# A graph attention layer on one core: the node stages at both ends in blocks of four, edge attributes by the pair, and the target rows as three bf16 parts in the one-hot product

## The chip, the cores and the metric

The kernel runs on one core of one Trainium2 chip. The metric is the device time of one execution in microseconds (us). All 400,000 edges and all 12,500 nodes are worked on by that one core, and every operand and result lies in the chip's DRAM before and after.

## The reference: what is computed

One pre-normalised graph attention layer with N = 12500 nodes, E = 400000 edges, C = 128 channels and H = 8 heads. The edges come sorted by their target `dst`. Cut to what matters:

```python
h = relu(layernorm(x))                                   # [N, 128]
msg = (h @ w_src + b_src)[src] + (h @ w_dst)[dst]         # [E, 128]
rad = mlp(edge_attr_32)                                  # 32 -> 64 -> 64 -> 128, silu between
m   = (msg * edge_weight1 * rad) @ w_sep + b_sep          # [E, 256]: per head 16 for alpha, 16 value
alpha = smooth_leaky_relu(m[.., :16]); value = m[.., 16:]
att = segment_softmax((alpha * alpha_dot).sum(-1), dst)  # per target node and head
out = segment_sum(value * att, dst)                       # [N, 128]
result = x + out @ w_proj + b_proj
```

## The kernel before

**Node stage** (L144 to L290). x is loaded in 7 groups of 14 blocks of 128 rows (97 full blocks and one of 84 rows). For each group, `stats` (L191) computes mean and variance on DVE and their scale and shift, `norm` (L204) makes h = relu(scale * x + shift) on ACT, and `products` (L212) takes four blocks at a time: PE transposes them (L220), DVE copies the transposes out (L223), PE multiplies each block with [w_src | w_dst] (L230), and two blocks at a time are evicted, the source half by an ACT copy (L237) and the target half by a DVE add that brings in b_src (L238). After 14 blocks the two halves are stored to the DRAM tables `t_src` and `t_dst` on SP's queue (L244). In the second group `ends_and_cuts` marks where neighbouring edges differ in their target, tests that the edges are sorted and the windows narrow (`bad`), and stores the sections' first and last targets. These come from four loads of 400 single words each, `base` and `last`, on SP's queue (L167, L168).

**Main loop** (`windows` L603, `passes` L644). The value `bad` is read back and the fast path is taken. `windows` loads the small MLP weights into block-diagonal tiles and computes `tgt`, `far`, `w_s` and `b_s`; then the edges go by in 400 pairs. A pair k is 1000 edges, two sections of 500, eight tiles of 125. All edges of a section have targets within 64 rows from its first one, its window. The order is written out by hand: `step(k)` issues the following, and each engine executes its own part in that order.

- Loads on SP: edge weights broadcast to 128 partitions (`load_w`, 500 KB) and the 64 target rows of each section's window (`load_md`, from `t_dst`) for pair k+3, targets of two pairs (`load_d`), edge attributes (`load_e`: 8 DMAs for 8 pairs, spread over the steps).
- `gather(k+4)`: eight indirect DMAs on POOL (L718), each fetching 125 rows of `t_src`. The tile `gs` has four buffers, so the gather for pair k+4 waits until the transposes of pair k (L770) have read theirs.
- `mlp3(k)`: PE L758 into `p3`, DVE L761 adds the bias and multiplies with the edge weight to `rad`.
- `message(k)`: PE transposes the gathered rows into the bank `pm` (L770) and adds the target rows onto it as a one-hot product, `md` [64 rows x 128] times `ohT` [64 x 500] in f32 (L775); DVE multiplies `pm` with `rad` to mT (L779).
- `alphas(k, 0)`, `alphas(k, 1)`: PE L783, ACT silu L785, DVE L787 give `al`, the alpha halves of the two sections.
- `values(c, f)` and `sums(c)` for the pair c = k - 12: PE L864 and DVE L866 weight the values with the softmax numerators, PE L875 sums them over the edges of each target into the bank `misc`, and ACT evicts it to `ob` (L879). `ob` is stored to `agg` (overlapping windows) and `win`.
- `mlp1(k+2)` (L736, L739), `mlp2(k+1)` (L744, L746), `one_hot_T(k+1)` (DVE L751), `e_T(k+3)` (L728, L730), and in every odd step `scores` (PE L794 into `misc`, ACT L797 to `Sp`) for two pairs. The softmax of eight pairs runs in the steps with k mod 8 = 1, 2, 3; the indices of 16 pairs are prepared in the steps with k mod 16 = 8.

The PSUM bank `misc` exists once and is shared by the indices, the scores, the softmax's transposes and the sums, so the scores of an odd step wait until ACT has evicted the sums before them. The value stage runs 12 pairs behind (LAG), and after pair 399 there are 14 more steps, in which the partial sums of targets that cross sections are combined and scattered to `agg` by indirect DMAs.

**Final stage** (L1126 to L1200). In 7 groups of 14 blocks: `agg` is loaded, POOL adds b_out to x (L1162), DVE computes the quotients (L1165 to L1168), PE transposes them (L1179), ACT copies them out (L1182), PE multiplies with w_proj (L1186), DVE adds a bias row where the node has edges (L1185) and then the sum to x (L1190), and the group is stored.

Of the kernel before, what the change touches and what calls it, by code (L numbers as in the profile page):

```python
# [53 lines left out]
EP = 8  # L54
# [3 lines left out]
def gnn_kernel(ctx: ExitStack, tc: tile.TileContext, a: dict, out: bass.AP):  # L58
# [18 lines left out]
    agg = dram.tile([N + W, ROW], F32, name="agg")  # L77
    win = dram.tile([NS * W, ROW], F32, name="win")
    base_d = dram.tile([2, NP], I32, name="base_d")
# [15 lines left out]
    x_v = x[0:NF * P, :].rearrange("(p t) c -> p t c", t=NF)  # L95
    ident = const.tile([P, P], F32, name="ident")
# [48 lines left out]
    with tc.tile_pool(name="node", bufs=2) as np_, tc.tile_pool(name="node1", bufs=1) as n1, \  # L145
# [6 lines left out]
        b_nodes = n1.tile([P, C], F32, name="b_nodes")  # L152
        nc.scalar.dma_start(out=b_nodes, in_=a["b_src"].to_broadcast([P, C]))
# [6 lines left out]
        last = n1.tile([1, 2, NP], I32, name="last")  # L160
# [3 lines left out]
        nc.sync.dma_start(out=prev[1:RP, :], in_=dst[RC - 1:E - 1].rearrange("(p c) -> p c", c=RC))  # L164
        with nc.allow_non_contiguous_dma(reason="the sections' ends"):
            for f in range(2):
                nc.sync.dma_start(out=base[:, f, :], in_=dst_h[f:f + 1, :, 0])  # L167
                nc.sync.dma_start(out=last[:, f, :], in_=dst_h[f:f + 1, :, SEC - 1])  # L168
# [16 lines left out]
        spans = groups[:-1] + [(groups[-1][0], NB)]  # L185
        hs = {}

        def rows(t):
            return P if t < NF else tail

        def stats(g):  # L191
            t0, t1 = spans[g]
# [11 lines left out]
        def norm(g):  # L204
            t0, t1 = spans[g]
            hs[g] = np_.tile([P, XG, C], F32, name="h")
            for t in range(t0, t1):
                n = rows(t)
                nc.scalar.activation(hs[g][:n, t - t0, :], x_all[:n, t, :], AF.Relu,
                                     bias=shift[:n, t:t + 1], scale=rstd[:n, t:t + 1])  # L210

        def products(g):  # L212
            t0, t1 = spans[g]
            ms = np_.tile([P, 2, XG, C], F32, name="ms")
            for u0 in range(t0, t1, 4):
                us = range(u0, min(u0 + 4, t1))
                pt = nps.tile([P, 4, P], F32, name="pt")
                for u in us:
                    n = rows(u)
                    nc.tensor.transpose(pt[:, u - u0, :n], hs[g][:n, u - t0, :], ident[:n, :n])  # L220
                hT = np_.tile([P, 4, P], F32, name="hT")
                w = (len(us) - 1) * P + rows(us[-1])
                nc.vector.tensor_copy(hT.rearrange("p u n -> p (u n)")[:, :w],  # L223
                                      pt.rearrange("p u n -> p (u n)")[:, :w])
                for v0 in range(0, len(us), 2):
                    vs = us[v0:v0 + 2]
                    pm = nps.tile([P, 2, 2, C], F32, name="pm", bufs=4)
                    for j, u in enumerate(vs):
                        n = rows(u)
                        nc.tensor.matmul(pm[:n, j], hT[:, u - u0, :n], w_nodes, start=True, stop=True)  # L230
                    i, m = vs[0] - t0, len(vs)
                    if rows(vs[-1]) == P:
                        cuts = [(P, 0, m)]
                    else:
                        cuts = [(P, 0, m - 1)] * (m > 1) + [(tail, m - 1, m)]
                    for n, j0, j1 in cuts:
                        nc.scalar.copy(ms[:n, 0, i + j0:i + j1, :], pm[:n, j0:j1, 0, :])  # L237
                        nc.vector.tensor_tensor(  # L238
# [999 lines left out]
```

## Time and profile before

| | us |
|---|---|
| runs of the kernel | 6549.27, 6550.76, 6562.26; median 6550.76 |
| profiled execution | 6566.2, its span 6564.2, mean granted TensorE clock 0.873 |
| start, up to the first gather | 0 to 215.9 |
| gathers | 215.9 to 6259 |
| last steps, combination, scatter | 6259 to 6417.7 |
| final stage | 6417.7 to 6564.2 |

The profile is of one execution. PE is TensorE (matmuls), PEld its weight loads, DVE VectorE, ACT ScalarE, POOL GpSimd and SP SyncE, which issues most DMAs here. A group of instructions is given by line, engine, operation, and the tiles it writes and reads; f32 matmuls appear as two records each, so that L775, two products in each step, has 1600 records for 400 pairs. "Idle before" is the time the engine stood still in front of an instruction, with the instruction whose signal ended it. The granted clock is a share of the full TensorE clock.

### The profile page before, as it was taken

What the parts mean: (1) busy time and instruction counts of PE and PEld (TensorE: products, weight loads), DVE (VectorE), ACT (ScalarE), POOL (GpSimd) and SP (SyncE); (2) the same over time, 40 slices, a digit from 0 to 9 for tenths busy, and PEclk for the clock granted to TensorE, in tenths of its full rate; (3) what the DMA queues carried; (4) which work ended last, traced back from release to release, by engine and by line L of the source; (5) the groups of instructions that cost most, each with busy time, mean ns of one, the idle gap of its engine ahead of it and who ended that gap; (6) DMA issues with size and microseconds to landing.
All of it is one profiled execution on the core that took longest, in us unless ns stands there. A gap on an engine that the chain in (4) does not pass through costs nothing. (4 is left out here: it accounts for less than half of the span.)

```text
span 6564.2 us, 79188 instructions
## 1 busy us (share of the span) xinstructions
PE 5066.2 (77%) x26490; PEld 2665.6 (41%) x26490; DVE 2887.1 (44%) x5210; ACT 1785.1 (27%) x3797; POOL 3111.5 (47%) x3231
## 2 busy tenths in 40 slices
PE   3477878787878878788788787887887878888774
PEld 2234444444444444444444444444444444444453
DVE  4234444444444444444444444444444444444465
ACT  3122222222222222222222222222222222222221
POOL 0455555455554545544455454454554545545402
PEclk7688898898998989988888898898888989888885
DMA  3454444444444444444444444444444444444423
GB/s 124 135 144 119 124 119 115 125 117 121 121 122 118 121 119 119 124 117 115 123 120 121 119 116 121 122 115 120 121 117 122 119 120 121 124 119 118 114 60 123
DMA packets 884920, 783.25 MB, mean 119 GB/s; under 512 B 527255, under 2 KB 773279, under 8 KB 884250
## 3 DMA queue, kind: packets, MB, share of 16 engines
q1 hardware_dynamic: 778482, 560.72, 31.0%
q0 software_dynamic: 102816, 210.37, 13.6%
q10 hardware_dynamic: 3202, 6.99, 0.3%
q8 instruction: 212, 3.47, 0.2%
q14 instruction: 208, 1.70, 0.1%
HBM read 643.82 MB, written 134.27 MB: 119 GB/s over the span
## 5 line engine op out<-in xcount | busy, mean ns | idle before, releaser
L718 POOL DMA_INDIRECT gs<-t_src,idx x3200 | 3067.4, 959 | 3189.3 <-PE pm L770 1756.2
L787 DVE SCALAR_TENSOR_TENSOR al<-pa,sl 128x500 f32<-128x500 f32 x800 | 542.9, 679 | 1570.9 <-ACT sl L785 1022.1
L761 DVE SCALAR_TENSOR_TENSOR rad<-p,c_fc_b,w_b 128x500 f32<-128x500 f32 x800 | 553.6, 734 | 1389.4 <-PE p L758 1102.0
L783 PE MATMUL pa<-mT,c_w_a 128*128 128x500 f32 x1600 | 833.7, 603 | 256.8 <-DVE mT L779 248.1
L785 ACT ACTIVATE sl<-pa,c_b_a 128x500 f32<-128x500 f32 x800 | 541.4, 677 | 1789.4 <-PE pa L783 626.9
L864 PEld LDWEIGHTS V<-c_w_v,mT 128*125 128x125 f32 x6208 | 741.2, 188 | 634.8 <-issue 337.9
L864 PE MATMUL V<-c_w_v,mT 128*125 128x128 f32 x6208 | 891.3, 286 | 23.2 <-issue 1.1
L794 PE MATMUL misc<-al,w_s 128*32 128x500 f32 x1600 | 365.9, 986 | 539.5 <-ACT ob L879 525.3
L779 DVE TENSOR_TENSOR mT<-pm,rad 128x500 f32<-128x500 f32 x800 | 504.3, 672 | 280.1 <-PE pm L775 252.8
L758 PE MATMUL p<-h,w3b 64*128 64x500 f32 x1600 | 625.5, 870 | 0.0
L770 PEld LDWEIGHTS pm<-ident,gs 125*128 125x128 f32 x3200 | 430.1, 169 | 435.9 <-issue 435.9
L866 DVE TENSOR_TENSOR pvx<-V,Pem 125x512 f32<-125x512 f32 x776 | 528.9, 682 | 44.4 <-PE m L744 26.5
L770 PE MATMUL pm<-ident,gs 125*128 125x125 f32 x3200 | 533.6, 321 | 0.0
L875 PEld LDWEIGHTS misc<-pvx,oh 125*64 125x64 f32 x6400 | 365.5, 137 | 322.4 <-issue 279.7
L875 PE MATMUL misc<-pvx,oh 125*64 125x136 f32 x6400 | 473.0, 287 | 28.2 <-DVE pvx L866 27.6
L783 PEld LDWEIGHTS pa<-mT,c_w_a 128*128 128x128 f32 x1600 | 269.5, 191 | 500.6 <-DVE mT L779 287.4
L775 PE MATMUL pm<-ohT,md 64*128 64x500 f32 x1600 | 471.0, 656 | 0.1
L739 ACT ACTIVATE h<-p,b 128x500 f32<-128x500 f32 x400 | 270.5, 676 | 700.9 <-PE pa L783 157.2
L879 ACT COPY ob<-misc 128x136 f32<-128x136 f32 x400 | 108.7, 272 | 1292.5 <-remote 630.5
L744 PE MATMUL m<-h,w2b 128*128 128x500 f32 x800 | 449.6, 644 | 0.0
L728 PE MATMUL m<-ident,e_t 125*128 125x125 f32 x800 | 187.4, 319 | 204.4 <-ACT h L746 169.8
L746 ACT ACTIVATE h<-m,b 128x500 f32<-128x500 f32 x400 | 270.7, 677 | 223.4 <-PE m L744 55.0
(145 smaller groups left out, 3153.1 us busy)
## 6 DMA issues: line engine op xcount, KB each, us to landing
w_b<-in_edge_weight SPq DMA_DIRECT2D x400, 500.0 KB
d_b<-in_dst SPq DMA_DIRECT2D x400, 250.0 KB
gs<-t_src,idx POOLq DMA_INDIRECT x3200
e_t<-in_edge_attr SPq DMA_DIRECT2D x400, 125.0 KB
sc_d<-Sp SPq DMA_DIRECT2D x200, 250.0 KB
win<-ob SPq DMA_DIRECT2D x400, 68.0 KB
agg<-ob SPq DMA_DIRECT2D x800, 33.5 KB
md<-t_dst SPq DMA_DIRECT2D x800, 32.0 KB
```

The lines of the kernel that those rows point to most:

```text
L718: nc.gpsimd.indirect_dma_start(out=gs[:, j, :], out_offset=None, in_=t_src[:, :], in_offset=bass.IndirectOffsetOnAxis(ap=idx[:, t:t + 1], ...
L758: nc.tensor.matmul(p3[:, f, 0:SEC], w3b[s, :], h2s[k][s, :], start=True, stop=True)
L761: nc.vector.scalar_tensor_tensor(rads[f], p3[:, f, 0:SEC], b3, w_g[k][:, f * SEC:(f + 1) * SEC], op0=ALU.add, op1=ALU.mult)
L770: nc.tensor.matmul(pm[f][:, t * T:(t + 1) * T], gs[:T, f * TS + t, :], ident[:T, :T], start=(t == 0), stop=False, is_transpose=True, skip_ ...
L775: nc.tensor.matmul(pm[f], md[k][s, :], ohT[k][s, :], start=False, stop=True, skip_group_check=True)
L779: nc.vector.tensor_mul(mTs[k][:, f * SEC:(f + 1) * SEC], pm[f], rads[f])
L783: nc.tensor.matmul(pa, w_a, mTs[k][:, f * SEC:(f + 1) * SEC], start=True, stop=True)
L785: nc.scalar.activation(sl, pa, AF.Silu, bias=b_a, scale=1.0)
L787: nc.vector.scalar_tensor_tensor(al, pa, 0.25, sl, op0=ALU.mult, op1=ALU.add)
L864: nc.tensor.matmul(V[:, t, :], mTs[c][:, o:o + T], w_v, start=True, stop=True)
L866: nc.vector.tensor_mul(pvx[c][:, f, :, 0:C].rearrange("p t (h k) -> p t h k", h=H), V.rearrange("p t (h k) -> p t h k", h=H), Pem[c // MP] ...
L875: nc.tensor.matmul(acc[f * W:(f + 1) * W, :], ohs[c][:, f * TS + t, :], pvx[c][:, f, t, :], start=(t == 0), stop=(t == TS - 1), skip_group ...
```

## The change

1. *Node stage.* 25 quads of four blocks. `norm(i+2)`, `turn(i+1)` (transposes and their copy) and `products(i)` are issued in this order; `stats` are made for eight blocks at a time. Two blocks are evicted in one copy with both halves, on ACT, and one pair in eight on DVE; b_src is no longer added. Each quad is stored by itself. The sections' first and last targets are loaded as 1600 words by one DMA into 100 partitions (`ends`); of the four loads of 400 words the two of `base` stay. The MLP weights, `w_s`, `b_s`, `tgt`, `far` and the final stage's bias row `v_out` are loaded or computed here. `fits` (the test and the stores of `ends`) runs after quad 12 and `cuts` after the last one.
2. *b_src in the message.* mT = (pm + b_src) * rad, one scalar_tensor_tensor instead of a product.
3. *Edge attributes.* One DMA for each pair, six steps ahead, four buffers. The four tiles' order in a section changes with it: h1 is written permuted and `rad` strided, in one tile of 1000 columns with one buffer.
4. *Target rows.* `ohT` is written in bf16. `md` is split one step ahead into three bf16 parts that sum to it exactly (`split_md`, two ACT copies and two DVE subtractions of 128x128), and the one-hot product is six bf16 matmuls instead of two f32 ones.
5. *x + b_out.* `load_x` and `add_x` compute it in the loop, a quad in every eighth step from step 40 on, and store it to a DRAM table `xb`.
6. *Final stage.* x comes from `xb`; quotients for 12 blocks at a time; `turn(i+1)` is issued ahead of `finish(i)`; the result is made in place and stored for each quad. POOL does nothing.

The diff, cut to its core:

```diff
-        last = n1.tile([1, 2, NP], I32, name="last")
+        ends = n1.tile([100, 8, 2], I32, name="ends")
...
                 nc.sync.dma_start(out=base[:, f, :], in_=dst_h[f:f + 1, :, 0])
-                nc.sync.dma_start(out=last[:, f, :], in_=dst_h[f:f + 1, :, SEC - 1])
+            nc.sync.dma_start(out=ends, in_=bass.AP(
+                at.tensor, at.offset, [[8 * SEC, 100], [SEC, 8], [SEC - 1, 2]]))
...
+        def norm(i):
+            t0, t1 = quads[i]
+            hs[i] = np_.tile([P, 4, C], F32, name="h", bufs=3)
...
+        def products(i):
+            t0, t1 = quads[i]
+            hT = hTs.pop(i)
+            ms = np_.tile([P, 2, 4, C], F32, name="ms", bufs=4)
+            for v0 in range(t0, t1, 2):
+                vs = range(v0, min(v0 + 2, t1))
+                pm = nps.tile([P, 2, 2, C], F32, name="pm", bufs=4)
+                for t in vs:
+                    n = rows(t)
+                    nc.tensor.matmul(pm[:n, t - v0], hT[:, t - t0, :n], w_nodes, start=True, stop=True)
+                for n, u0, u1 in blocks(v0, vs[-1] + 1):
+                    o, q = ms[:n, :, u0 - t0:u1 - t0, :].rearrange("p k j c -> p j k c"), pm[:n, u0 - v0:u1 - v0]
+                    if v0 % 16 == 2:
+                        nc.vector.tensor_copy(o, q)
                     else:
-                        nc.scalar.copy(ms[:n, 0, i + j0:i + j1, :], pm[:n, j0:j1, 0, :])
-                        nc.vector.tensor_tensor(
-                            ms[:n, 1, i + j0:i + j1, :], pm[:n, j0:j1, 1, :],
-                            b_nodes[:n].unsqueeze(1).to_broadcast([n, j1 - j0, C]), op=ALU.add)
+                        nc.scalar.copy(o, q)
             f1 = min(t1, NF)
             for k, table in enumerate((t_src, t_dst)):
                 tv = table[0:NF * P, :].rearrange("(p t) c -> p t c", t=NF)
-                nc.sync.dma_start(out=tv[:, t0:f1, :], in_=ms[:, k, 0:f1 - t0, :])
+                if t0 < f1:
+                    nc.sync.dma_start(out=tv[:, t0:f1, :], in_=ms[:, k, 0:f1 - t0, :])
...
+        for i in range(Q):
+            if i % 2 == 0 and 4 * i + G < NB:
+                stats(4 * i + G, min(4 * i + 2 * G, NB))
+            if i + 2 < Q:
+                norm(i + 2)
+            if i + 1 < Q:
+                turn(i + 1)
+            products(i)
+            if i == 12:
+                fits()
+        cuts()
...
-            def load_e(g, i):
...
+            def load_e(k):
+                e_g[k] = lp.tile([T, 8, RAD], F32, name="e_t", bufs=4)
+                nc.sync.dma_start(out=e_g[k], in_=ea_t[k])
...
+            def split_md(k, i):
+                if i == 0:
+                    m3[k] = lp.tile([P, 3, C], BF16, name="m3")
+                    nc.scalar.copy(m3[k][:, 0, :], md[k])
+                elif i == 1:
+                    mr[k] = lp.tile([P, C], F32, name="mr")
+                    nc.vector.tensor_sub(mr[k], md.pop(k), m3[k][:, 0, :])
+                elif i == 2:
+                    nc.scalar.copy(m3[k][:, 1, :], mr[k])
+                else:
+                    nc.vector.tensor_sub(m3[k][:, 2, :], mr.pop(k), m3[k][:, 1, :])
...
-                nc.scalar.activation(h1s[k].rearrange("p (q e) -> p q e", q=2), p1[:, :, 0:2 * T],
+                nc.scalar.activation(h1s[k].rearrange("x (f q p) -> x q f p", f=2, q=2),
+                                     p1[:, :, 0:2 * T].rearrange("x q (f p) -> x q f p", f=2),
...
-                ohT[k] = sp.tile([P, SEC], F32, name="ohT")
+                ohT[k] = sp.tile([P, SEC], BF16, name="ohT")
...
-                rads = [sp.tile([C, SEC], F32, name="rad", bufs=3) for _ in range(2)]
...
+                rad = sp.tile([C, PR], F32, name="rad", bufs=1)
+                v = "x (t h p) -> x h t p"
+                n = dict(t=4, h=2)
+                for h in range(2):
+                    nc.vector.scalar_tensor_tensor(
+                        rad.rearrange(v, **n)[:, h], p3[:, h, 0:SEC].rearrange("x (t p) -> x t p", t=4),
+                        b3, w_g[k].rearrange(v, **n)[:, h], op0=ALU.add, op1=ALU.mult)
...
-                for f in range(2):
-                    s = slice(f * W, (f + 1) * W)
-                    nc.tensor.matmul(pm[f], md[k][s, :], ohT[k][s, :], start=False, stop=True,
-                                     skip_group_check=True)
+                for j in range(3):
+                    for f in range(2):
+                        s = slice(f * W, (f + 1) * W)
+                        nc.tensor.matmul(pm[f], m3[k][s, j, :], ohT[k][s, :], start=False, stop=(j == 2),
+                                         skip_group_check=True)
...
-                    nc.vector.tensor_mul(mTs[k][:, f * SEC:(f + 1) * SEC], pm[f], rads[f])
+                    s = slice(f * SEC, (f + 1) * SEC)
+                    nc.vector.scalar_tensor_tensor(mTs[k][:, s], pm[f], b_n, rad[:, s], op0=ALU.add, op1=ALU.mult)
...
+                if has(k + 6) and k >= -4:
+                    load_e(k + 6)
...
+                i, q = divmod(k - 40, MP)
+                if 0 <= i < Q and q == 5:
+                    load_x(i)
+                if 0 <= i < Q and q == 7:
+                    add_x(i)
                 if has(k + 4):
                     gather(k + 4)
+                if has(k + 1):
+                    split_md(k + 1, 0)
                 if has(c):
                     sums_begin(c)
                 if has(k):
                     message(k, mlp3(k))
                 if has(c):
                     values(c, 0)
+                if has(k + 1):
+                    split_md(k + 1, 1)
                 if has(k):
                     alphas(k, 0)
+                if has(k + 1):
+                    split_md(k + 1, 2)
                 if has(c):
                     values(c, 1)
...
                     one_hot_T(k + 1)
+                    split_md(k + 1, 3)
...
-                nc.gpsimd.tensor_tensor(x_all[:n, t0 + a0:t0 + a1, :], x_all[:n, t0 + a0:t0 + a1, :],
-                                        b_out[:n].unsqueeze(1).to_broadcast([n, a1 - a0, C]), op=ALU.add)
...
+        for i in range(Q):
+            if i % 3 == 0 and i // 3 + 3 < NG:
+                load_g(i // 3 + 3)
+            if i % 3 == 1 and i // 3 + 1 < NG:
+                quotients(i // 3 + 1)
+            if i + 1 < Q:
+                turn(i + 1)
             finish(i)
```

## The prediction, made before the changed kernel was run

> **What bounds the kernel now.** The page's first part names no engine that is full:
>
> ```profile
> PE 5066.2 (77%) x26490; PEld 2665.6 (41%) x26490; DVE 2887.1 (44%) x5210; ACT 1785.1 (27%) x3797; POOL 3111.5 (47%) x3231
> ```
>
> PE is the busiest at 77%, so the first question is whether PE's work sets the step. The costliest groups (busy us, mean ns, then the idle time before them) and the waits say otherwise:
>
> ```profile
> L718 POOL DMA_INDIRECT gs<-t_src,idx x3200 | 3067.4, 959 | 3189.3 <-PE pm L770 1756.2
> ...
> L775 PE MATMUL pm<-ohT,md 64*128 64x500 f32 x1600 | 471.0, 656 | 0.1
> ```
>
> ```profile
> POOL gs L718 <- PE pm L770: 1756.2, 235, 11.7
> ...
> ACT ob L879 <- remote: 630.5, 181, 4.7
> ...
> PE misc L794 <- ACT ob L879: 525.3, 144, 4.3
> ```
>
> POOL does nothing in the loop but issue gathers, is busy 3067 us and waits for the transposes of `message` (L770) 1756 us. PE in its turn waits 525 us at the scores (L794) for `ob`, the eviction of the sums' bank, and `ob` waits for something "remote" or for PE lines that have nothing to do with it. The timeline of two steps (start, duration, engine, line; in brackets the idle time and its releaser) shows the circle:
>
> ```profile
> 3003.91 0.27 ACT L879 COPY ob<-misc 128x136 f32<-128x136 f32 x1 [3.11 <-remote]
> ...
> 3004.23 1.90 PE L794 MATMUL misc<-al,w_s 128*32 128x500 f32 x8 [3.52 <-ACT ob L879]
> ...
> 3006.06 2.04 PE L758 MATMUL p<-h,w3b 64*128 64x500 f32 x4
> ...
> 3008.03 1.93 PE L770 MATMUL pm<-ident,gs 125*128 125x125 f32 x8
> ...
> 3009.89 1.11 PE L775 MATMUL pm<-ohT,md 64*128 64x500 f32 x4
> 3010.23 0.94 POOL L718 DMA_INDIRECT gs<-t_src,idx  x1 [8.16 <-PE pm L770]
> ...
> 3018.96 0.94 POOL L718 DMA_INDIRECT gs<-t_src,idx  x1 [0.30 <-issue]
> ...
> 3021.63 0.27 ACT L879 COPY ob<-misc 128x136 f32<-128x136 f32 x1 [4.34 <-PE pm L775]
> ...
> 3022.24 0.95 POOL L718 DMA_INDIRECT gs<-t_src,idx  x1 [2.34 <-PE V L864]
> ...
> 3028.51 1.15 PE L875 MATMUL misc<-pvx,oh 125*64 125x136 f32 x16
> ...
> 3033.76 0.27 ACT L879 COPY ob<-misc 128x136 f32<-128x136 f32 x1 [2.32 <-remote]
> ```
>
> Eight gathers are issued from 3010.23 to 3019.90 and eight from 3022.24 on; the next batch of POOL starts at 3041.34. The sums (L875) are on PE's record at 3028.51 to 3029.66, yet `ob` starts at 3033.76, 1.8 us after the last gather (3031.92). At 3021.63 it is again 1.7 us after a last gather. Only then can the scores start, after 3.5 us without PE work, then p3 and the transposes, 1.9 to 2.0 us each, and then POOL. So a pair of steps is two batches of 9.7 us and two gaps: 2.3 us after an even batch and 7.0 to 9.4 us after an odd one (1.8 to `ob`, 0.3 `ob`, 1.90 scores, 2.04 p3, 1.93 transposes, 0.3 to the first gather = 8.3). Whatever makes PE's signals arrive so late while gathers are issued, it goes away with them. The windows (busy us and records for PE, PEld, DVE, ACT, POOL; clock; DMA):
>
> ```profile
> 216.00:6259.00 6043.00, 4806.08 (x25206) 2470.80 (x25206) 2613.28 (x4602) 1679.93 (x3529) 3067.25 (x3200) 0.89 0.47 121
> 6275.00:6304.00 29.00, 28.20 (x176) 15.53 (x174) 18.29 (x33) 8.64 (x20) 0.18 (x1) 1.00 0.08 24
> ```
>
> From 6275 to 6304 no gather is issued, `ob` follows the sums by 0.05 us, and three steps take 10.1, 10.4 and 8.6 us with PE 97% busy. In the 6043 us of the loop a step takes 15.1 us. So a step with gathers has some 5 us that PE's work doesn't fill: **the loop is bound by the gathers and by the chain ob, scores, p3, transposes; PE's other work lies beside POOL's batch.** The two ends are different. The node stage, 62 to 210:
>
> ```profile
> L230 PE MATMUL pm<-w_nodes,hT 128*128 128x256 f32 x144 | 49.5, 499 | 52.8 <-DVE hT L223 52.8
> ...
> L209 ACT ACTIVATE h<-x_all,shift,rstd 128x128 f32<-128x128 f32 x55 | 21.6, 480 | 2.3 <-DVE shift L201 2.3
> L238 DVE TENSOR_TENSOR ms<-pm,b_nodes 128x256 f32<-128x256 f32 x36 | 14.9, 423 | 60.0 <-ACT ms L237 60.0
> ```
>
> There each engine waits for the next one (58 us, 66 us, 36 us busy of 148): a group of 14 blocks takes 24.1 us (115.1, 139.1, 163.2), 6.9 us for four blocks. The final stage, 6417.7 to 6564.2:
>
> ```profile
> L1185 DVE SCALAR_TENSOR_TENSOR x_fin<-v_out,has,x_fin 128x128 f32<-128x128 f32 x97 | 49.1, 564 | 0.0
> ...
> L1162 POOL TENSOR_TENSOR x_fin<-x_fin,c_b_out 128x1792 f32<-128x1792 f32 x6 | 25.6, 4285 | 9.4 <-DVE r L1165 9.3
> ```
>
> While POOL adds b_out (29.3 us in all), four STTs of DVE take 7.68 to 8 us for two to four of them; without it four take 1.13 us. Later a group of 14 takes 17.1 us, DVE and PE in turn.
>
> **The change, part by part.** The sum is made against the profiled execution: 6566.2 us, span 6564.2, which is 15.4 us above the runs' median.
>
> *Start.* Before, the first gather is at 215.9. For a quad of four blocks after: ACT four norms at 0.39 (21.6 / 55), 1.75 copies of 128x512 at 0.585 (the qT copy of the final stage), half an rstd 0.15: 2.75 us. DVE four stats (0.26 + 0.18), one hT copy 0.68, a quarter copy 0.17, 0.2 for rstd and shift: 2.8 us. PE 12 operations: 1.6 us warm, 3.1 us at low clock. With turns and norms issued ahead these overlap: some 3.0 us a quad, 75 us in all, instead of 6.9. But the stores are on SP's queue, and SP is not free: `base` and `last` (four loads of 400 single words) hold it for 3.0 + 10.1 + 13.8 + 14.3 us until 60.3. Of the four, two stay (13 us), one load of 1600 words comes, and 14 loads of weights move here from the preamble (7.3 us there). The 1600 words cost between 3 us (100 partitions share them) and 55 (four times the last row); I take 41, what the same 1600 words cost now, so SP is free at 19.1 + 13 + 41 + 8.8 = 82. Four `ms` buffers let four quads run ahead; 21 more at 3.0 end at 145; 3 for the last store, 8 for `cuts` (sm 3.5 + 1.0, far 1.0, tgt, small ones), 9.5 for the index loads, transposes and first gather: 165.5. **Saving 50 us, between 25 and 85.**
>
> The stores become 50 of 256 KB instead of 14 of 0.9 MB. The row nearest to it: in 62 to 210 DMA engines are 24% busy and stores are not what PE or ACT wait for. The Trainium skill ("DMA: Bandwidth & Descriptors", section "Bandwidth") speaks against it: batch transfers to 1 MiB or more. By the fit in the same page's section "Anatomy of one DMA — SWDGE (gpsimd) path", 2.0 us plus bytes at 436 GB/s, 50 stores one after the other would take an estimated 130 us where 14 take 58, which would eat the saving; no row here shows them one after the other.
>
> *Loop, PE.* L775 is 4 records in 1.11 us; after, 6 records. Price from both sides: half of today's, -0.55 us, or six records at today's 0.28 each, +0.55. Which, matters little: the product starts 0.3 us before POOL's first gather and the next thing that POOL or the scores need is 9.7 us off. I take 0 on the path. The cover is the POOL batch: if it were gone, the price would be 400 times this, 220 us down or up. In the four steps behind the last gather it counts: 2 us saved. (By the skill's "TensorE: Matmul & The Clock Gate", section "Back-to-back issue gap", a pass of 500 columns takes 0.21 us, so three passes of two side-by-side halves are an estimated 0.63 us, and one after another 1.27; the row here is 1.11 for the f32 form.)
>
> *Loop, ACT and DVE.* Two copies of 128x128 (0.27, the L237 row of that shape) and two subtractions (0.29, the L238 row) for each step; 0.5 us on ACT and 0.6 on DVE, which are 27% and 44% busy. `md` is issued three steps ahead and read a step earlier than now, two steps (30 us) after its issue. The first copy stands before `pvx`, and Sp and eT stand before it. The second copy waits for DVE's subtraction, and h1 and h2 are queued behind it on ACT; they feed PE beside the gathers. mT as STT instead of a product: 679 against 672 ns (rows L787, L779). rad written strided, h1 permuted: nothing to twice their 1.38 and 0.68 us, all behind POOL's start. Path: 0.
>
> *Loop, DMAs.* e_t has as many bytes, one issue per step instead of 8 per 8 steps. 25 loads and 25 stores of 256 KB for `xb` add 13 MB to 783 MB; SP waits at each store for one DVE add (0.69 us), which stands where DVE idles for p3 (5.96 us above); the stores behind it wait that long. Path: 0, up to 25 us for the 25.
>
> *End.* POOL's adds go. DVE per quad: four STTs 1.13, add 0.69, and quotients 3.17 us per 14 blocks, so 0.91: 2.73. PE per quad 1.8 warm to 3.2 cold. 25 quads: 68 to 80 us, I take 74; 12 for the first load and quotients, 4 for the last store: 90 against 146.5. **Saving 56, between 40 and 70.**
>
> Sum: 6566.2 - 50 - 56 - 2 = 6458; minus 15.4: **6443 us**.
>
> **Rivals.** *A: PE's time does count.* For it: 77% busy, and POOL's releaser is now and then PE V L864 or L775, lines behind the product, in 156 of 400 batches. If `ob` and POOL's start move with PE's work, 0.55 us for 400 steps go: 6443 - 220 = 6223. Against it: the fixed 1.8 us after the last gather, at both parities.
>
> *B, slower: alpha comes after ob.* The scores need al(k,1), whose STT ends at 3032.15 in the odd step, 1.6 us ahead of `ob`; nearly always the later one is `ob` (144 of 200). The two copies, two subtractions and their hops all stand ahead of sl and al in ACT's and DVE's queues. If they delay al by more than 1.6 us, the rest is paid in each of 200 pairs of steps; from 1.6 + 106/200 = 2.1 us on it eats both ends. At 3 us: 6443 + 280 = 6723. Against: the work itself is 1.1 us.
>
> *C: SP keeps the start.* The 1600 words take 55 us or more, and stores in quads take turns: saving 25 instead of 50, 6468.
>
> *D: the ends don't gain*, since PE stays at low clock and each quad keeps the present pace: the start then saves only the shorter preamble (some 10 us) and the end POOL's adds (some 25): 6516.
>
> **Chances.** Forecast 0.70, A 0.10, B 0.09, C 0.06, D 0.05. 0.2% is 13 us, about what a measurement of this kernel tells from no change. Range: low, all savings at their ends (85 + 70 + 25 for the one step in eight where POOL starts right with the transposes) give 6371, and a little of A: 6350; high, savings of 25 and 40 give 6488, with the 25 us of `xb`'s stores 6513. A and B stay outside, with 0.19. Faster 0.89, same 0.03 (a mild B, a bad D), slower 0.08.
>
> **What would show it.** First gather near 165 and final stage near 90 us; POOL's batches still 9.7 us with gaps near 2.3 and 8 us; `ob` still 1.7 to 1.8 us after the last gather; the bf16 product under 1.11 us with PE's busy time down and the loop still near 6040 us. I am wrong if the loop's length moves by more than 30 us, if PE's wait at L794 is put down to al, or if SP's first store of t_src is behind 100.

## The result and the profile after

The changed kernel takes 6388.68 us (median of 4 runs, 6373.5 to 6407.9) against 6552.52 us (4 runs, 6549.3 to 6562.3): 0.9749 of the time, 95% interval 0.972 to 0.9778. The forecast was 6443 us, its range worked out as 6350 to 6513. The profiled execution took 6386.36 us, its span 6384.3. Its stages beside those of the profile before:

| us | before | after | change | forecast |
|---|---|---|---|---|
| start to first gather | 215.9 | 159.8 | -56 | -50 |
| first gather to end of the last | 6043.0 | 5979.6 | -63 | 0 |
| to the load of x in the final stage | 158.9 | 158.0 | -1 | -2 |
| final stage | 146.5 | 86.9 | -60 | -56 |

Both ends came as worked out. The loop did not: it got 63 us shorter between these two executions. Taken from the medians, 164 us less the 117 of the other rows, it is some 47. Most of the rest of this document is about those.

The runs of this study were made on several chips, and the same program is not equally fast on them: on some the kernel before takes 6552 to 6630 us, as here, on others 4924 to 4926. They are called the late and the punctual chips below, for a reason that the traces show; times are compared as ratios to the kernel before on the same chip. Where a ratio from one chip is set against a ratio from another, it is taken for granted that the ratio of each kernel is the same on both, which between two late chips was not measured.

Part 1 of the page after, the costliest groups and the waits, in the order of those shown before:

```profile
PE 4973.4 (78%) x27292; PEld 2659.9 (42%) x27292; DVE 3111.7 (49%) x6006; ACT 1951.4 (31%) x4595; POOL 3094.4 (48%) x3223
```

```profile
L739 POOL DMA_INDIRECT gs<-t_src,idx x3200 | 3079.9, 962 | 3057.3 <-PE pm L796 1632.3
...
L802 PE MATMUL pm<-ohT,m 64*128 64x500 bf16 x2400 | 357.3, 387 | 23.5 <-issue 22.8
```

```profile
POOL gs L739 <- PE pm L796: 1632.3, 215, 12.9
...
PE misc L822 <- ACT ob L907: 426.7, 146, 4.5
...
ACT ob L907 <- remote: 360.9, 164, 4.8
```

PE's busy time fell by 93 us, DVE's and ACT's rose by 225 and 166. The one-hot product is 357 us on PE's record instead of 471. PE still waits for `ob` at the scores, 427 us instead of 525. The timeline of an even step (start, duration, engine, line, idle time and releaser):

```profile
3008.07 0.94 POOL L739 DMA_INDIRECT gs<-t_src,idx  x1 [9.63 <-PE pm L796]
...
3011.68 0.69 PE L758 MATMUL p<-eT,w1b 64*128 64x250 f32 x4
...
3014.18 1.15 PE L903 MATMUL misc<-pvx,oh 125*64 125x136 f32 x16
...
3014.81 0.68 ACT L761 ACTIVATE h<-p,b 128x500 f32<-128x500 f32 x1 [3.43 <-issue]
...
3016.88 0.94 POOL L739 DMA_INDIRECT gs<-t_src,idx  x1 [0.30 <-issue]
...
3017.67 0.68 PE L749 MATMUL m<-ident,e_t 125*128 125x125 f32 x2 [2.34 <-ACT h L769]
...
3019.91 0.27 ACT L907 COPY ob<-misc 128x136 f32<-128x136 f32 x1 [1.58 <-remote]
...
3022.45 0.94 POOL L739 DMA_INDIRECT gs<-t_src,idx  x1 [4.63 <-PE pm L796]
```

The batch of eight gathers runs from 3008.07 to 3017.82, and POOL goes on at 3022.45. `ob` starts 4.6 us after the recorded end of the sums (3015.33) and 2.1 us after the last gather. It looks like the picture before, with one thing that the forecast passed over: h1 (L761) needs p1 (L758), whose record ends at 3012.37, and h1 starts at 3014.81; only then come h2 and e_T (L749, at 3017.67, waiting for h2). So here it is not only the sums, at the end of the batch, that come late. The loop as a whole (busy us and records of PE, PEld, DVE, ACT, POOL; clock; DMA):

```profile
159.80:6139.50 5979.70, 4748.28 (x25998) 2488.92 (x25998) 2878.93 (x5422) 1838.62 (x4323) 3079.95 (x3200) 0.88 0.49 124
```

At the start, SP's queue holds the load of 1600 words for 13.65 us and the first weights, behind it, for 17.97; the first store of t_src leaves at 70.99 (forecast 82):

```profile
33.03 13.65 SPq L177 DMA_DIRECT2D ends<-in_dst  x1
46.81 17.97 SPq L189 DMA_DIRECT2D w1b<-in_fc_w  x2
...
70.99 0.52 SPq L266 DMA_DIRECT2D t_src<-ms  x1
```

In the final stage the 97 STTs take 27.5 us where they took 49.1 beside POOL's adds:

```profile
L1253 DVE SCALAR_TENSOR_TENSOR x_fin<-v_out,has,x_fin 128x128 f32<-128x128 f32 x97 | 27.5, 345 | 0.0
```

### The profile page after: what moved, and what is told of

The parts are those of the page before. It is cut to its first block, busy times and chain, and to the rows that moved or that the text cites. A ratio compares the mean times of both kernels' runs of the same rounds, so it can differ in the third digit from the quotient of the medians.

```text
span 6384.3 us, 83248 instructions
## 1 busy us (share of the span) xinstructions
PE 4973.4 (78%) x27292; PEld 2659.9 (42%) x27292; DVE 3111.7 (49%) x6006; ACT 1951.4 (31%) x4595; POOL 3094.4 (48%) x3223
## 4 chain that ended last, share of the span: by engine, by line
PE 49%; DVE 8%; another core or an unknown queue 6%; issue 4%; ACT 3%; DMA 1%; SPq 1%; ACTq 0%; DVEq 0%
PE V L892 7%; PE pa L811 7%; PE p L781 6%; PE pm L796 5%; PE misc L903 5%; PE m L767 5%; PE pm L802 4%; PE misc L822 4%; DVE rad L786 3%; PE p L758 3%; DVE mT L807 2%; PE m L749 2%; DVE pvx L894 1%; ACT h L769 1%
## 5 line engine op out<-in xcount | busy, mean ns | idle before, releaser
L811 PE MATMUL pa<-mT,c_w_a 128*128 128x500 f32 x1600 | 878.1, 632 | 326.1 <-DVE mT L807 270.6
L892 PEld LDWEIGHTS V<-c_w_v,mT 128*125 128x125 f32 x6208 | 796.1, 197 | 578.5 <-issue 293.0
L892 PE MATMUL V<-c_w_v,mT 128*125 128x128 f32 x6208 | 947.8, 296 | 84.0 <-issue 37.3
L822 PE MATMUL misc<-al,w_s 128*32 128x500 f32 x1600 | 349.1, 936 | 443.9 <-ACT ob L907 426.7
L807 DVE SCALAR_TENSOR_TENSOR mT<-pm,c_b_n,rad 128x500 f32<-128x500 f32 x800 | 553.5, 733 | 233.9 <-PE pm L802 138.1
L781 PE MATMUL p<-h,w3b 64*128 64x500 f32 x1600 | 604.7, 842 | 0.0
L761 ACT ACTIVATE h<-p,b 128x500 f32<-128x500 f32 x400 | 271.8, 679 | 670.7 <-PE p L758 189.1
L802 PE MATMUL pm<-ohT,m 64*128 64x500 bf16 x2400 | 357.3, 387 | 23.5 <-issue 22.8
L749 PE MATMUL m<-ident,e_t 125*128 125x125 f32 x800 | 181.6, 311 | 187.7 <-ACT h L769 142.9
```

The source lines that it names most:

```text
L781: nc.tensor.matmul(p3[:, f, 0:SEC], w3b[s, :], h2s[k][s, :], start=True, stop=True)
L802: nc.tensor.matmul(pm[f], m3[k][s, j, :], ohT[k][s, :], start=False, stop=(j == 2), skip_group_check=True)
L807: nc.vector.scalar_tensor_tensor(mTs[k][:, s], pm[f], b_n, rad[:, s], op0=ALU.add, op1=ALU.mult)
L811: nc.tensor.matmul(pa, w_a, mTs[k][:, f * SEC:(f + 1) * SEC], start=True, stop=True)
L822: nc.tensor.matmul(ps[32 * j:32 * j + 32, :], w_s, als.pop(2 * k - 2 + j), start=True, stop=True)
L892: nc.tensor.matmul(V[:, t, :], mTs[c][:, o:o + T], w_v, start=True, stop=True)
```

## The experiments

**The f32 product, without and with the split (late chip).** Two theories: the gathers still set the pace and PE's clock explains the gain, or PE's time counts after all.

```diff
-                ohT[k] = sp.tile([P, SEC], BF16, name="ohT")
+                ohT[k] = sp.tile([P, SEC], F32, name="ohT")
...
-                for j in range(3):
-                    for f in range(2):
...
-                        nc.tensor.matmul(pm[f], m3[k][s, j, :], ohT[k][s, :], ...)      # bf16
+                for f in range(2):
...
+                    nc.tensor.matmul(pm[f], md[k][s, :], ohT[k][s, :], ...)              # f32
...
-                    split_md(k + 1, 0)   # and 1, 2, 3: gone in the first, kept in the second
```

> The changed kernel with the old one-hot product (f32, two products, no split of md); everything else of the change stays. The changed kernel's loop (first gather to end of the last) took 5979.6 us against 6043.0 before, and two theories explain the 63 us. Clock theory: the gathers still set the pace, but the split's work on ACT and DVE delays PE's last operations of a step, so PE stands still 2.9 us before the scores instead of 3.7, and scores, p3 and transposes run less often at low clock (scores 1.75 instead of 1.83 us on the mean). PE theory: the product is shorter (357 against 471 us busy) and that time goes through to the loop. Both expect the loop back near 6030 to 6045 us, +50 to +65 us in the time; the clock theory with PE's idle time before the scores back near 3.6 us, the PE theory with that idle time as in the changed kernel.

> As the run with the f32 product, but the split of md (two copies on ACT, two subtractions on DVE a step) is still done and not used. Clock theory: the split's delay is what counts, so the loop stays near 5980 us (within 25), PE's idle time before the scores near 2.9 us. PE theory: the product is as long as before, so the loop is at 6030 to 6090 us, +50 to +110 us against the changed kernel.

Measured: without the split 6515.7 us, 0.9856 of the kernel before (0.9826 to 0.9885); with the split 6614.5 us, 0.9996 (0.9972 to 1.002). The changed kernel is at 0.9749. So the product alone (second run against the changed kernel) saves 0.0247, 163 us of the 6614 on this chip, and the split alone (second against first) costs 0.014, 93 us, each give or take some 25 us. The split's price comes from one chip (the medians differ by 99 us, the profiled loops, 6100.5 and 6222.3 us, by 122). The product's rests on the changed kernel's ratio from another chip; what there is on this chip agrees: the next run but one, the changed kernel with three idle products more, takes 191 us less than the f32 product with the split. The clock theory expected the second run near the changed kernel, so that theory is out. The PE theory expected 50 to 110 us from the product; it was more, and a price of the split, which the forecast and both theories had at nothing, gives more than half of it back.

**The product done twice (late chip).**

```diff
-                for j in range(3):
+                for j in range(6):
...
-                        nc.tensor.matmul(pm[f], m3[k][s, j, :], ohT[k][s, :], start=False, stop=(j == 2), ...)
+                        nc.tensor.matmul(pm[f], m3[k][s, j % 3, :], ohT[k][s, :], start=False, stop=(j == 5), ...)
```

> The changed kernel with the three bf16 products done twice (12 instead of 6 a step; the target rows count double in the message). PE gets 0.8 us more a step, behind POOL's start. Clock theory: hidden beside the gathers, the loop is at 5980 us or up to 60 us shorter, since PE's work ends later and its idle time before the scores falls below 2.9 us. PE theory: the loop grows by some 0.8 us a step where PE counts, +100 to +320 us.

Measured: 7184.5 us, 1.083 (1.0788 to 1.0873), 0.108 above the changed kernel: 715 us of 6614, 1.8 us a step for six products which PE's record shows at 0.6 to 0.7 us. (The changed kernel's ratio is again that of another chip; the 191 us found above without it are of the size of the 163 by ratios, so 715 can't come from that.) Both theories had too little. The timeline of a step:

```profile
3004.38 0.69 PE L758 MATMUL p<-eT,w1b 64*128 64x250 f32 x4
...
3006.87 1.15 PE L903 MATMUL misc<-pvx,oh 125*64 125x136 f32 x16
...
3008.81 0.68 ACT L761 ACTIVATE h<-p,b 128x500 f32<-128x500 f32 x1 [4.74 <-PE misc L903]
3008.88 0.94 POOL L739 DMA_INDIRECT gs<-t_src,idx  x1 [0.30 <-issue]
...
3011.79 0.27 ACT L907 COPY ob<-misc 128x136 f32<-128x136 f32 x1
```

p1 ends on record at 3005.07 and h1, which waits for nothing else by then, starts at 3008.81. Over the loop h1 starts 9.5 and 9.4 us (medians of even and odd batches) after POOL's first gather, 5.9 and 6.6 with the f32 product on the same chip, and 4.4 and 5.8 in the changed kernel's first profile, while p1's records end between 4.3 and 5.5. **On a late chip PE's results come later than its record, and later still when PE is given six products more.** `ob` is then 2.55 us behind the last gather on the median (1.8 to 3.7 for nine in ten), where it was 1.8.

But PE's own load isn't all that moves it. With the unused split, which gives PE nothing to do, h1 starts at 7.2 us at both parities, though p1's records end at 4.6 and 5.1 us (4.6 and 4.8 without the split) and ACT stood idle ahead of h1 for longer, 1264 us in all instead of 1050. Where the lost time enters the loop can be read from a wait of PE, that of the attributes' transposes (e_T, L749) for h2, with the f32 product, with the f32 product and the split, and with the product twice:

```profile
PE m L749 <- ACT h L769: 298.4, 221, 5.0
PE m L749 <- ACT h L769: 493.2, 241, 13.6
PE m L749 <- ACT h L769: 834.9, 300, 5.2
```

The transposes of e_T share the PSUM bank `m1` with p2, so they can't start until h2 has read it, and p3 and the message's transposes, on which POOL waits, stand behind them on PE. In the changed kernel's first profile this wait is 142.9 us. In the same order the scores' wait for `ob` is 353, 285 and 121 us, so it shrinks. With the split the two waits together grow by 127 us, and the loop by 122. POOL's mean gap behind an even batch, where no scores stand, is 2.9, 3.6 and 5.9 us (2.5 in the changed kernel), behind an odd one 8.1, 8.0 and 8.7 (7.7), with batches of 9.7 to 9.8 us throughout.

**PE kept busy ahead of the scores (late chip).**

```diff
                 if has(k) and k % 2 == 1:
+                    if has(c) and c < NP - LAG:
+                        V = pp.tile([T, TS, C], F32, name="V")
+                        for i in range(3):
+                            nc.tensor.matmul(V.rearrange("p t c -> p (t c)")[:, 0:SEC], mTs[c][:, 0:T],
+                                             mTs[c][:, 0:SEC], start=True, stop=True)
                     scores(k)
```

> The changed kernel with three idle products (f32, 125x128 by 128x500, into the V bank, which nobody reads) ahead of the scores in every odd step: some 3 us of PE work in the 3 us in which PE stands still. Clock theory: scores, p3 and transposes run at the full clock (1.05, 1.11 and 1.07 us instead of 1.75, 1.87 and 1.50 on the mean), 1.9 us less in each of 200 pairs of steps that wait for the scores, less what the idle products overrun: the loop is 150 to 350 us shorter. PE theory: 3 us of PE work more for two steps, longer by 0 to 200 us. A third possibility, that the lower clock at this place has nothing to do with the idle time before it, expects scores still near 1.75 us and no gain.

Measured: 6423.6 us, 0.9701 (0.9672 to 0.973); the interval overlaps the changed kernel's, so the gain of some 30 us isn't clear of noise. The timeline from `ob` to POOL:

```profile
3000.72 0.27 ACT L907 COPY ob<-misc 128x136 f32<-128x136 f32 x1 [1.76 <-remote]
...
3001.33 1.05 PE L822 MATMUL misc<-al,w_s 128*32 128x500 f32 x8
...
3002.30 1.11 PE L781 MATMUL p<-h,w3b 64*128 64x500 f32 x4
...
3003.34 1.07 PE L796 MATMUL pm<-ident,gs 125*128 125x125 f32 x8
...
3004.69 0.95 POOL L739 DMA_INDIRECT gs<-t_src,idx  x1 [5.70 <-PE pm L796]
```

The scores, p3 and transposes do run at the full clock, 1.05, 1.11 and 1.07 us, 1.06, 1.12 and 1.08 on the mean instead of 1.75, 1.87 and 1.50. But on the mean the scores start 2.1 us after `ob`, not 0.8. From the start of an odd batch to the next one, with the scores in between, it is 17.3 us on the mean, 17.9 with the f32 product on this chip and 17.6 in the changed kernel's profile; from an even batch to the next one 13.0, 12.6 and 12.4. What the clock gave, the idle products and the other half of the pair took. (The Trainium skill, "TensorE: Matmul & The Clock Gate", section "Part 1: The HAM clock gate", has the clock halved after at least one idle window of about 3.4 us. The scores took 1.90 us behind 3.52 us without PE work in the profile before and 1.05 us with the gap filled, which agrees; but in the timeline of the changed kernel PE's record has a gap of only 2.34 us ahead of L749, and the granted clock is 0.50 from 3018 to 3022 us, so there a shorter gap on record was enough.) So PE's recorded idle time ahead of the scores was no free time to fill.

**The changed kernel on a punctual chip.**

> The changed kernel itself, on the chip of the following runs, so that their traces can be compared on one chip. By the ratio measured first (0.975) it should take 0.975 of the kernel before; the runs with the f32 product and with the product done twice were made on a chip where the kernel before took 6614 us instead of 6552, and there it should have been near 6448.

Measured: 4759.4 us, 0.9663 of 4925.8 (0.9648 to 0.9678). Page, window of the loop and timeline at the end of the sums:

```profile
PE 4367.0 (92%) x27292; PEld 2417.9 (51%) x27292; DVE 3135.0 (66%) x6006; ACT 1983.2 (42%) x4595; POOL 3125.6 (66%) x3223
```

```profile
158.50:4520.90 4362.40, 4148.81 (x26004) 2252.23 (x26004) 2901.99 (x5422) 1870.84 (x4325) 3111.22 (x3200) 0.99 0.72 170
```

```profile
2512.43 1.15 PE L903 MATMUL misc<-pvx,oh 125*64 125x136 f32 x16
...
2513.63 0.27 ACT L907 COPY ob<-misc 128x136 f32<-128x136 f32 x1 [0.35 <-PE misc L903]
```

Same program, same gathers, 0.94 us each on the median, batches of 9.9 us on the mean. But `ob` starts 0.05 us after the sums' recorded end, at the 5th as at the 95th percentile of all steps, and 2.5 us (median) ahead of the end of the last gather. PE is busy 92% of the span and 95% of the loop, whose steps take 10.9 us; the clock is 0.99. So here the loop is bound by PE, openly, and gathers alone don't make PE's results late.

**Half the gathers, and half with the product twice (punctual chip).**

```diff
-                for j in range(8):
+                for j in range(4):
                     t = k % 16 * 8 + j
...
-                        nc.tensor.matmul(pm[f][:, t * T:(t + 1) * T], gs[:T, f * TS + t, :],
+                        nc.tensor.matmul(pm[f][:, t * T:(t + 1) * T], gs[:T, t, :],
```

> The changed kernel with four instead of eight gathers a step; the second section of a pair uses the first one's rows (half of the gathering is left out). POOL's batch falls from 9.8 to 4.8 us. Cover theory (the prediction's): PE's signals are held back until the last gather plus 1.8 us, so the sums' eviction comes at the end of PE's own work, 7.3 us behind the batch's start instead of 11.5; a pair of steps falls from 30.1 us by some 8, the loop to 4300 to 4700 us. PE theory: PE's own work is what takes 11.5 us, gathers or not; the loop stays above 5700 us.

> As the run with half the gathers, with the three bf16 products done twice. With all gathers the doubling cost 1.8 us a step where PE's record shows 0.6 to 0.7 us more. If PE is slowed only while gathers are under way, the doubling costs little more than its record here, 250 to 350 us for 400 steps. If the six additional products are that slow by themselves, it costs 600 us or more again.

Measured: 4739.8 us with half the gathers, 0.9622 (0.9607 to 0.9637), 20 us under the changed kernel; a step takes 10.86 us on the mean with batches of 4.7 as it took 10.91 with batches of 9.9. POOL merely waits longer (last column the longest wait):

```profile
POOL gs L739 <- PE pm L796: 2439.3, 394, 13.0
```

The gathers cost this loop next to nothing. With the product twice it takes 4956.0 us, 1.0064 (1.0048 to 1.0079): 216 us more, 0.54 us a step, where PE's record has 576 instead of 323 us, 0.63 us a step. That is what it costs if PE is the bound and its record true. On the late chip the same six products cost 1.8 us, there with all gathers. The comparison thus changes chip and gathers at once: the product done twice with all gathers on a punctual chip, and half the gathers on a late one, were not run. That it is the chip is argued from the 20 us that half the gathers are worth here.

**The scores one step later (punctual chip).**

```diff
-                if has(k) and k % 2 == 1:
-                    scores(k)
...
                     message(k, mlp3(k))
+                if has(k - 1) and k % 2 == 0:
+                    scores(k - 1)
```

> The changed kernel with the scores of an odd step issued in the next step, behind the transposes and the target rows' product of that step instead of ahead of them. PE then need not wait for the sums' eviction before p3 and the transposes, on which POOL waits. If the chain last gather, eviction, scores, p3, transposes sets the even steps, their gap falls from 7.9 to some 2.5 us: 200 times 5 us, the loop is 800 to 1100 us shorter. If PE's own work behind the gathers sets the pace, only the 2.3 us without PE work and the low clock after them are saved: 300 to 700 us. If neither, less than 100 us.

Measured: 4748.0 us (4740 to 4754, all under the changed kernel's 4758 to 4761), 0.9642 (0.9629 to 0.9655). 11 us, the last of the three cases. Of the versions that leave nothing out it is the fastest here on a punctual chip.

**The split made once, in the node stage (punctual chip).**

```diff
+    t_d3 = dram.tile([N + W, 3, C], BF16, name="t_d3")     # written per quad: copy, subtract, copy, subtract
...
-                    nc.sync.dma_start(out=md[k][f * W:(f + 1) * W, :], in_=t_dst[ds(at[f], W), :])
+                    nc.sync.dma_start(out=m3[k][f * W:(f + 1) * W], in_=t_d3[ds(at[f], W)])
...
-                    split_md(k + 1, 0)   # and 1, 2, 3
```

> The changed kernel with the three bf16 parts made once in the node stage and stored as a table of 768-byte rows, from which the windows' rows are loaded; the four operations of the split leave the loop (400 times two ACT copies and two DVE subtractions of 128x128) and come into the node stage (25 times the four of 128x512: 1.2 us on ACT and 1.4 us on DVE a quad). In the run with the f32 product and the unused split the split cost 99 us of the loop on its chip. If that price is what the split costs where it stands, the loop gets 60 to 100 us shorter and the start 20 to 40 us longer: 0.96 to 0.968 of the kernel before, against 0.966 to 0.975 for the changed kernel. If ACT's and DVE's load in the loop costs nothing and the 99 us had another cause, it is slower than the changed kernel by the 20 to 40 us.

Measured: 4778.5 us, 0.9711 (0.9697 to 0.9724), 19 us slower than the changed kernel on the other punctual chip. The first gather is 27 us later (185.9), with operations such as this one on DVE,

```profile
L266 DVE TENSOR_TENSOR m3n<-rn,m3n 128x512 bf16<-128x512 f32 x22 | 15.0, 683 | 0.2 <-ACT m3n L264 0.2
```

and the loop is 9 us shorter (4353.8 against 4362.4). The second case: on a punctual chip the split in the loop costs next to nothing. On a late chip, where it cost 93 us, this version was not run.

**The f32 product again, without and with the split (punctual chip).**

> The run with the f32 product again, to see whether its price is the same on another chip. If PE's record is the whole truth, as on the chip of the run with half the gathers (PE 92% busy, signals on time), the f32 product costs 0.30 us a step more than the bf16 one (1.11 against 0.81) and the missing split gives back what it costs; with both ends saving 117 us, a loop as long as before means 0.976 of the kernel before on a chip where that takes 4926 us, and 0.986 as measured where it takes 6614.

> The run with the f32 product and the unused split again, beside the former one on the same chip. The two differ by the split alone: 0.010 to 0.015 of the kernel before if its price is 70 to 100 us on every chip, nothing if ACT and DVE hide it where PE's signals are on time. Against the changed kernel it differs by the product alone: 120 us by PE's record, 166 us where it was measured first.

Measured: 4845.8 us, 0.9843 (0.9828 to 0.9858), and 4853.5 us, 0.9856 (0.9841 to 0.9871); the kernel before took 4923.5. So here the split costs some 8 us, and the product saves 94 us (4853.5 to 4759.4; the two chips agree on the kernel before within 3 us). PE's record says 122, from the groups of the f32 run and of the changed kernel:

```profile
L801 PE MATMUL pm<-ohT,md 64*128 64x500 f32 x1600 | 445.0, 632 | 0.7 <-DMA md<-t_dst 0.7
```

```profile
L802 PE MATMUL pm<-ohT,m 64*128 64x500 bf16 x2400 | 323.2, 375 | 0.0
```

The f32 version was expected at 0.976 and is at 0.984: its loop, 4445 us, is some 43 us longer than an estimate of the loop before on such a chip (4925 less the 523 us that the profile before has outside the loop). That profile is of a late chip; the changed kernel has 407 us outside the loop in its late profile and 398 in its punctual one, so 34 us may be nearer. By this estimate something else of the change costs there; no run shows what.

**b_src by PE in the node stage, with the later scores (late chip).**

```diff
-                    nc.tensor.matmul(pm[:n, t - v0], hT[:, t - t0, :n], w_nodes, start=True, stop=True)
+                    nc.tensor.matmul(pm[:n, t - v0], hT[:, t - t0, :n], w_nodes, start=True, stop=False)
+                    nc.tensor.matmul(pm[:n, t - v0], ones[0:1, :n], b_row, start=False, stop=True)
...
-                    nc.vector.scalar_tensor_tensor(mTs[k][:, s], pm[f], b_n, rad[:, s], op0=ALU.add, op1=ALU.mult)
+                    nc.vector.tensor_mul(mTs[k][:, s], pm[f], rad[:, s])
...
```

> The run with the scores issued later, and b_src no longer added in the message: in the node stage PE adds it with one more product per block (a row of ones times b_src), and mT is a plain product again. The loop of the changed kernel with the f32 product (4445 us where signals are on time) is some 43 us longer than the loop of before can be there (4925 us less the 523 us outside the loop), so something else that the change brings into the loop costs. If it is mT, 733 instead of 672 ns twice a step, ahead of the pvx for which PE waits at V, this loop is 40 to 50 us shorter than the 4350 us of the run with later scores, and the start 0 to 15 us longer: 0.955 to 0.959 of the kernel before on such a chip. If the cost lies elsewhere (edge attributes by the pair, permuted writes, x + b_out), the loop stays within 15 us of 4350 and the ratio near 0.964.

Measured: 6589.5 us, 0.9947 (0.9922 to 0.9971), on a late chip, so it doesn't answer what it was made for. The first gather is at 287.2 us, 127 later than in the changed kernel. PE is busy for 225.5 of the 247 us from 40 us on, and the added products of one row take it as long as those of 128 rows (window of the node stage):

```profile
L259 PE MATMUL pm<-b_row,ones 1*128 1x256 f32 x180 | 109.6, 710 | 0.0
L258 PE MATMUL pm<-w_nodes,hT 128*128 128x256 f32 x178 | 105.2, 695 | 0.0
```

Those of 128 rows have become longer too: in the changed kernel 152 of their records from 40 to 160 us keep PE busy for 41.3 us, at a mean granted clock of 0.73, here 178 take 105.2 at 1.00. There is no gather in this stage. Whether it is the mix of the two forms or the chip, no run tells.

The loop is 6093 us in the profile. Scaled to the median it is near 6060, what the changed kernel would have there at its ratio, so the plain mT and the later scores together gained nothing on this chip; whether mT's 733 instead of 672 ns are the 34 to 43 us of the punctual chips stays open.

## Why the prediction was right, and where it was wrong

**Start: right, the terms less so.** Quads took 3 to 3.5 us. SP was free at 71 instead of 82, since the 1600 words over 100 partitions held it 13.65 us, between the 3 and the 55 that bounded it; but the weights' loads took 24 us there, not 8.8, the first two 18 of them. The errors cancel, which was luck. The 50 smaller stores showed no sign of costing what they would one after the other: from 82 us on a pair of them leaves SP every 2 to 5 us and holds it 0.75 us, and no engine waits for one. The rule of the Trainium skill ("DMA: Bandwidth & Descriptors", section "Bandwidth") to batch transfers to 1 MiB or more did not bind here, and the estimated 130 us were not seen.

**End: right.** DVE's STTs lost the time that POOL's adds had cost, and the quads take the pace that was worked out (87 against 90 us).

**Loop: wrong in its reading.** The step that failed is "I take 0 on the path" for the product, and with it "Path: 0" for the split. Both rested on one observation, `ob` 1.8 us behind the last gather at both parities, from which it was concluded that everything behind POOL's start is covered by the batch. The runs on late chips show that it is not: work added there lengthens the loop, by more than it takes on PE's record (product twice: 715 us), while the batches stay as long. On a punctual chip, with as many gathers, the lateness is absent and the loop is PE's. By its own sign the forecast was wrong about the loop, which moved by 63 us where 30 were allowed. The other signs came true, and told nothing: in the changed kernel too `ob` is 1.74 us behind the last gather and the gaps are 2.35 and 7.95 us (medians). The first profile had a warning in it: in about a third of its steps h1, too, starts over 0.5 us behind p1's recorded end, not only the sums behind theirs.

**The sizes.** On late chips the product is worth -163 us, inside the -0.55 us a step that bounded it (-220), and the split +93, where its work was counted (1.1 us a step) and its path put at 0. Sum -70 us, against -47 to -63 for the whole loop. On punctual chips it is -94 and +8, with some +34 to +43 for the other edits in the loop by the estimate above. The ends gave what was forecast, 117 us of the 164; for the loop the forecast held because what it lost and gained nearly cancels, and that was luck. (A slip in the range: savings of 25 and 40 us give 6486 us, not 6488; nothing rests on it.)

**The rivals.** A was right that PE's time counts, and lacked the split's price; 0.10 was too little for it. B was right that the split can cost, but not about the place: the scores start 0.71 us after `ob` on the mean with the split and 0.74 without, and PE's wait for `ob` falls. The wait that grows is that for h2, in the very queue that the forecast named ("h1 and h2 are queued behind it on ACT") and then put at 0. C and D did not happen.

**Open.** Why PE's results come late on some chips. The mean granted clock there is 0.85 to 0.88 and on the punctual chips 0.97 to 0.98, but with PE kept busy it was 0.925 and the results were as late, and in the timeline of the changed kernel it is 1.00 from 3008 to 3016 us, where h1 starts 2.4 us behind p1's record; so the recorded clock alone isn't it. In the last steps of the first profile, without gathers, they were on time, but there the DMA engines were at 0.08 instead of 0.47 as well, so the gathers and the other loads can't be told apart. And why h1 comes later with the split, when PE has no more to do, no run took apart.

## What to carry to other kernels

A consumer that starts microseconds after its producer's recorded end is a sign that the producer is not done, so the idle time behind that record is not cover: first see whether other consumers of the same engine are late as well, and whether the delay moves when work is added to that engine or to its neighbours. A sign that both readings expect decides nothing. Price an edit that replaces work on one engine by work on two others as two terms, with one run for each; here -163 and +93. And measure both on the chip on which the result counts: the same split cost 93 us on one and some 8 on another.

## What the hardware did that was not expected

The same program took 4926 us on some chips and 6552 to 6630 on others, with gathers equally long (0.94 us on the median) and the sums' eviction 0.05 or 4.0 us (median) behind PE's record. A product over one row took as long as one over 128 beside it (710 and 695 ns a record at 128x256). Six bf16 products of 64x500 cost 0.54 us on a punctual chip with half the gathers and 1.8 us on a late one with all of them.
